# ScalarE issues the query/key weight loads and the gated stores, a SiLU moves behind the next copy, and one routing product is cut in two

## The chip, the cores and the metric

The kernel runs on one core of a Trainium2 chip. The metric is the device time of one execution in microseconds (us), lower is better. A profiled execution also gives a span, from the first to the last instruction that the profiler recorded; the time of that same execution is a little longer than its span.

## The reference, cut to what matters

All numbers are float32. The input `x` is 2 batches of 512 tokens with 512 features. A layer norm gives `xn`, and the output is

```
x + attention(xn) + mixture(xn)
attention: qkv  = silu(xn @ qkv_w.T)            # 32 heads, head size 128, q, k and v
           out  = a decayed linear attention: within a block  (q k^T * decay) v,
                  between blocks                              (q * q_decay) state,
                  state = state * block_decay + (k * k_decay)^T v
           gate = sigmoid(xn @ gate_w.T)
           y    = (gate * norm_w * out / rms(out)) @ out_w.T
mixture:   xn @ W_base.T + b_base, plus eight rank-16 experts, of which each token
           uses the two with the largest router value
```

## The kernel before, in words

**Stages.** A short setup normalises and transposes the tokens, computes the router and most of the base product, and prepares sums of input blocks. A long middle part, from about 26 us to about 940 us of the span, computes the four projections (v, gate, q, k) and, in its second half, the attention itself. The last part multiplies the gated attention with `out_w`.

**The projections are a two-level seven-product scheme.** A product of 2x2 blocks is made of 7 products of block sums instead of 8 products of blocks, and each of those 7 is again split into 7. One outer product is called a round, and it is one entry of the list `rounds`; one inner product is one slot, so that a round has seven slots. The list `SLOTS` says which inner product stands in which slot: `((0, 1), (0, 5), (1, 7), (0, 2), (0, 6), (0, 3), (1, 4))`. The first number tells whether it belongs to the current round or to the one before, the second is the number of the inner product. A slot costs TensorE about 0.86 us. Round kinds 0 and 1 compute v and gate; kind 2 computes queries and keys, for four heads in a set of weights. A set has seven rounds.

**What the other engines do for a round.** Inner product 1 is accumulated in the PSUM tile `pa` (a bank of the pair `fr`). Then ScalarE copies it to the tile `pb` (L558, `sd<-ps_fr` in the profile), because product 2 will be added on top of `pa` and product 6 on top of `pb`. Product 5 is made in `pc`, in the other bank of its pair. After product 6 ScalarE copies `pb` to `pd` (L569, `sd<-sd`), and VectorE takes `w` from `pb` (L552). Products 2, 3, 7 and 4 each end in an addition on VectorE (L537), whose result goes to an outer sum (`sum`) or, where the outer sum is complete, to the result itself. For queries and keys the result is the tile `qk`, and the function `result` then applies SiLU on ScalarE (L514), and calls `complete` when the item (one head of one batch) has all it needs.

**The attention of an item** is written as a generator, `attend`, and runs in pieces that the main loop starts in certain slots (`later`, `stage`): load v (L691), transpose keys by blocks on VectorE (L697, L698), store them to DRAM (L702, `k_kept`) and load them back in another layout by four loads (L707, `kt`), make the scores (L715, L720, L724), load the gate (L731), scale the keys on ScalarE (L736, `kd`), make the state (L739 to L746), make the output in PSUM and gate it (L756, `gT`), square it (L763, `sq`), and store it (L766, `g_kept`).

**The order is written by hand.** The middle part lies in a manual schedule: every engine executes its instructions in the order in which the Python code emits them, and each waits by semaphores for what it needs. SyncE (SP) has hardly any other work than to issue DMAs: each DMA is an instruction in its queue. Eight semaphores are shared by all DMAs, and each DMA waits for the earlier one on its own semaphore.

**Weight loads.** `load_block` fills a tile `raw` (five buffers) with two DMAs of 256 KB each, and the main loop takes one of them in every second slot of some rounds:

```
weights = load_blocks(n + 1, *{5: ((0, 0),), 7: ((1, 0), (1, 1)), 3: ((0, 1),)}.get(q, ()) ...)
if m % 2 == 0:
    next(weights, None)
```

The order within a slot is: weight load, delayed pieces (`later`), the piece of `stage`, the inner product of the slot, and then `after`, which emits the copies and additions that follow it.

Of the kernel before, what the change touches and what calls it, by code (L numbers as in the profile page):

```python
# [36 lines left out]
AF = mybir.ActivationFunctionType  # L37
# [5 lines left out]
P = 128  # L43
# [18 lines left out]
def attn_moe_kernel(ctx: ExitStack, tc: tile.TileContext, x, qk_w, v_w, gate_w, out_w, norm_w,  # L62
# [79 lines left out]
    def load_block(n, fo, ko):  # L142


        t = blocks[n, fo, ko] = aw.tile([P, 2, 2, 256], F32, tag="raw", name="raw", bufs=5)
        ks = slice(2 * ko, 2 * ko + 2)
        for i in range(2):
            if kind(n) == 0:
                nc.sync.dma_start(t[:, i], v_w[n - n % 2 + i][:, ks, fo * 256 : (fo + 1) * 256])
            elif kind(n) == 1:  # L150
                h = 4 * (n - n % 2) + 4 * i + 2 * fo
                nc.sync.dma_start(t[:, i], gate_w[h : h + 2, :, ks, :].rearrange("f p k d -> p f (k d)"))
            else:
                nc.sync.dma_start(t[:, :, i, :],
                                  qk_w[4 * (n - VG) + 2 * fo + i][:, :, ks, :].rearrange("p u k d -> p u (k d)"))
            yield

    def load_blocks(n, *of):
# [276 lines left out]
    def inner_product(o, r, i, first):  # L435
        n, q = rounds[r]
        a = operand[n, q][i]
        x_ = {1: xo[q][:, 0, :HB], 2: xo[q][:, 1, :HB], 3: xo[q][:, 1, HB:], 4: xt[q - 1][:, 3],
              5: xt[q - 1][:, 0], 6: xt[q - 1][:, 1], 7: xt[q - 1][:, 2]}[i]
        for u in range(2):  # L440
            if kind(n) == 0:

                mm(o.rearrange("p (g j d) -> p j g d", g=2, j=2)[:, u], x_[:, u * P : (u + 1) * P], a,
                   first and u == 0, True, turned=u, skip_group_check=True)
            else:
                mm(o[:, u * HB : (u + 1) * HB], a[:, u], x_, first and u == 0, True, skip_group_check=True)
# [59 lines left out]
    def result(n, fo, to, ij, v):  # L506

        fi, ti = divmod(ij, 2)
        if kind(n) < 2:
            g = pass_result(n, fo, to, ij, v)  # L510
            for slots in (3, 4):
                later[now[0] + slots].append(g)
            return
        nc.scalar.activation(v, v, AF.Silu)  # L514
        if ij in (1, 2):
            complete((4 * (n - VG) + 2 * fo + fi, to))

    def after(r, i):

# [66 lines left out]
    def route():  # L586

        f = work.tile([P, 4, NT, NE], F32, tag="squares", name="squares", bufs=2)
        g = work.tile([P, 8, NT], F32, tag="kd", name="kd", bufs=2)
        lg, prio, hit1, hit2 = (f[:, i] for i in range(4))  # L590
        c1, m1, m2, c2, w1, w2 = (g[:, i] for i in range(6))
        hl = moe["hl"] = ring("qk", [P, NT, NE, R])
        nc.sync.dma_start(lg, routed[:, :, :NE])
        nc.sync.dma_start(hl, routed[:, :, NE:].rearrange("p t (e r) -> p t e r", e=NE))
        yield

        for e in range(NE):
            nc.gpsimd.memset(prio[:, :, e : e + 1], float(NE - e))

        def wide(v):  # L600
            return v.unsqueeze(2).to_broadcast([P, NT, NE])

        def largest(m, c, hit):
            nc.vector.tensor_reduce(m, lg, AX.X, ALU.max)
            yield
            nc.vector.tensor_tensor(hit, lg, wide(m), ALU.is_equal)
            yield
            nc.vector.tensor_tensor(hit, hit, prio, ALU.mult)
            yield
            nc.vector.tensor_reduce(c, hit, AX.X, ALU.max)  # L610
            yield
            nc.vector.tensor_tensor(hit, hit, wide(c), ALU.is_equal)
            yield

        yield from largest(m1, c1, hit1)
        nc.vector.scalar_tensor_tensor(lg, hit1, LOWEST, lg, ALU.mult, ALU.add)
        yield
        yield from largest(m2, c2, hit2)

        nc.vector.tensor_tensor(w2, m1, m2, ALU.subtract)  # L620
        nc.scalar.activation(w2, w2, AF.Tanh, scale=0.5)
        for _ in range(4):
            yield
        nc.vector.tensor_scalar(w1, w2, SCALING / 2, SCALING / 2, ALU.mult, ALU.add)
        nc.vector.tensor_scalar(w2, w2, -SCALING / 2, SCALING / 2, ALU.mult, ALU.add)
        yield
        nc.vector.tensor_tensor(hit1, hit1, wide(w1), ALU.mult)
        yield
        nc.vector.tensor_tensor(hit2, hit2, wide(w2), ALU.mult)
        yield  # L630
        nc.vector.tensor_tensor(hit1, hit1, hit2, ALU.add)
        yield
        hl = hl.rearrange("p t e r -> p (t e) r")
        nc.vector.tensor_tensor(hl, hl, hit1.rearrange("p t e -> p (t e)").unsqueeze(2).to_broadcast([P, NT * NE, R]),
                                ALU.mult)

    def transpose_experts():

# [38 lines left out]
    def complete(item):  # L677

        items.append(item)
        g = running[len(items) - 1] = attend(*item)  # L680
        ready[len(items) - 1] = now[0] + 4
        for slots in (1, 2, 3, 6):
            later[now[0] + slots].append(g)

    def attend(head, b):
# [77 lines left out]
            nc.scalar.activation(sq, pa, AF.Square)  # L763
            nc.gpsimd.tensor_tensor(ssq[b], ssq[b], sq, ALU.add)  # L764
        yield
        nc.sync.dma_start(g_kept[head // 2][:, :, head % 2, b, :], gT.rearrange("p (f s) -> p f s", f=2))  # L766
        yield

    running = {}
# [124 lines left out]
    for k in range(7 * len(rounds) + 7):  # L894
        now[0] = k
        r0, m = divmod(k, 7)
        if m == 0:
            if r0 == 3:
                routing = route()
            if r0 == 15:  # L900
                for slots, g in zip((2, 5, 11, 18), 4 * [transpose_experts()]):
                    later[k + slots].append(g)
            if r0 == 50:
                zero_scores()
            if 20 <= r0 < 40:
                next(laying)
            if r0 in range(18, 18 + 3 * NT, 3):
                for slots, g in zip((0, 8, 11, 13), 4 * [experts((r0 - 18) // 3)]):
                    later[k + slots].append(g)
            if r0 + 2 < len(rounds):  # L910
                coming = encode(*rounds[r0 + 2])
            if r0 < len(rounds):
                n, q = rounds[r0]
                state_of[r0] = {}
                for _, to in ADDED[q]:
                    if to == "u3":
                        outer_sums[n, to] = outer_sums[n, "u2"]
                    elif isinstance(to, str):
                        if (n, q) == (1, 1):

                            t = [ring("qk", [P, 2, 512]) for _ in range(2)]
                            outer_sums[n, to] = [t[ij // 2][:, ij % 2] for ij in range(4)]
                        else:
                            t = aw2.tile([P, 4, 512], F32, tag="sum", name="sum", bufs=3)
                            outer_sums[n, to] = [t[:, ij] for ij in range(4)]
                weights = load_blocks(n + 1, *{5: ((0, 0),), 7: ((1, 0), (1, 1)), 3: ((0, 1),)}.get(q, ())
                                      if n + 1 < NSET else ())
        next(more_sums, None)

        if (r0, m) == (3, 0) or r0 in (5, 11, 12, 13):  # L930
            next(routing, None)
        if m % 2 == 0:
            next(weights, None)

        for g in later.pop(k, ()) if k != 7 * len(rounds) + 5 else ():
            next(g)
        begin_output(k - 7 * len(rounds))
        if r0 == len(rounds) and SLOTS[m][0] == 0:
            if m == 0:
                sums[0].update({1: bank("fr"), 6: bank("fr"), 5: seeded[0], 7: seeded[1]})  # L940
            early_product()
        begun = None
        if items:
            credit = min(credit + 24 / 49, 1.5)
            if credit >= 1:
                begun = next(stage)
        back, i = SLOTS[m]
        r = r0 - back
        if 0 <= r < len(rounds):
            st = state_of[r]  # L950
            if i in (1, 5):
                st["pa" if i == 1 else "pc"] = bank(
                    "at" if i == 5 and rounds[r] == (VG, 7) else "fr" if kind(rounds[r][0]) == 2 or i == 1 else "sc")
            inner_product(st[{1: "pa", 2: "pa", 5: "pc", 3: "pc", 6: "pb", 7: "pd", 4: "pd"}[i]], r, i, i in (1, 5))
            after(r, i)
        if r0 + 2 < len(rounds):
            next(coming, None)
        if begun is False:
            next(stage)
            credit -= 1  # L960
# [206 lines left out]
```

## Time and profile before

| | |
|---|---|
| three timed runs | 1118.1, 1119.52 and 1120.59 us, median 1119.52 us |
| profiled execution | 1121.18 us, its span 1119.4 us |
| mean granted TensorE clock | 0.998 |
| busy, share of the span | TensorE (PE) 1106.9 us, 99%; VectorE (DVE) 773.3 us, 69%; ScalarE (ACT) 444.9 us, 40%; GpSimd (POOL) 765.7 us, 68% |
| DMA issues by SP | 949, of which 64 are the query/key loads (L154) and 64 the `g_kept` stores (L766) |
| moved by DMA | 201.09 MB, mean 180 GB/s |

In the profile PE is TensorE's matrix multiply, PEld its weight load, DVE is VectorE, ACT is ScalarE, POOL is GpSimd and SP is SyncE; an engine's name with a q behind it is its instruction queue (its sequencer). L154 means line 154 of the kernel. Tile names stand without buffer numbers, `out<-in`. TensorE's busy time is modelled and matmuls overlap, so its waits are better read from the start times of successive products than from the busy share.

### The profile page before, as it was taken

How to read it: one execution, taken by the hardware profiler on the slowest of the kernel's cores; microseconds unless marked ns; L12 is line 12 of the kernel's file. 1: busy time of each engine (PE TensorE's matmuls, PEld its weight loads, DVE VectorE, ACT ScalarE, POOL GpSimd, SP SyncE). 2: the span in 40 equal slices, each digit the busy share in tenths (PEclk: the TensorE clock that was granted, in tenths of full speed). 3: DMA queues.
4: the chain of work that ended last, by engine and by line, in shares of the span. 5: the costliest groups of instructions: out<-in, count | busy, mean ns of one | idle time of the engine just before them, and what ended most of it. 6: DMA issues, size and time to landing. Idle time of an engine off the chain costs nothing.

```text
span 1119.4 us, 30341 instructions
## 1 busy us (share of the span) xinstructions
PE 1106.9 (99%) x11984; PEld 849.9 (76%) x11984; DVE 773.3 (69%) x1535; ACT 444.9 (40%) x842; POOL 765.7 (68%) x825
## 2 busy tenths in 40 slices
PE   8999999999999999999999899999999999999998
PEld 7666777777777777777777678777777877777776
DVE  8777776676766668787877777778777786535424
ACT  4344444434444444444444443535444443410000
POOL 3568778779768776677687676777777667545542
PEclk9999999999999999999999999999999999999999
DMA  5534576776743546665665666657666677944221
GB/s 178 156 114 159 163 241 202 220 229 209 239 143 132 177 146 197 182 199 154 199 187 160 191 183 186 189 164 211 181 197 177 211 234 233 350 132 127 86 90 57
DMA packets 190925, 201.09 MB, mean 180 GB/s; under 512 B 53696, under 2 KB 163008, under 8 KB 190656
## 3 DMA queue, kind: packets, MB, share of 16 engines
q1 hardware_dynamic: 190640, 199.03, 57.9%
q8 instruction: 95, 1.56, 0.6%
q14 instruction: 46, 0.38, 0.1%
q10 hardware_dynamic: 144, 0.13, 0.0%
HBM read 128.79 MB, written 75.55 MB: 183 GB/s over the span
## 4 chain that ended last, share of the span: by engine, by line
PE 79%; DVE 10%; DMA 4%; issue 3%; ACT 3%; SPq 1%; POOL 1%; DVEq 0%; ACTq 0%; POOLq 0%
PE sd L99 28%; PE ps_fr L99 24%; PE ps_sc L99 17%; PE ps_at L99 8%; PE ps_sc L715 2%; DVE qk L537 2%; DVE sum L537 2%; DMA raw<-in_qk_w 1%; ACT sd L569 1%; ACT qk L514 1%; DVE w L552 1%; DMA k_kept<-squares 1%; DMA v<-v_kept 1%; DVE gT L756 1%; DVE y L552 0%
## 5 line engine op out<-in xcount | busy, mean ns | idle before, releaser
L99 PE MATMUL sd<-xt,e 128*64 128x256 f32 x1344 | 175.8, 379 | 0.0
L764 POOL TENSOR_TENSOR ssq<-ssq,sq 128x512 f32<-128x512 f32 x62 | 79.2, 1277 | 138.0 <-ACT sq L763 131.0
L514 ACT ACTIVATE qk<-qk 128x512 f32<-128x512 f32 x128 | 80.3, 630 | 203.5 <-DVE qk L537 203.5
L99 PEld LDWEIGHTS sd<-xt,e 128*64 128x64 f32 x1344 | 102.6, 137 | 35.3 <-issue 2.6
L552 DVE TENSOR_TENSOR w<-sd,sum 128x512 f32<-128x512 f32 x110 | 74.5, 690 | 61.0 <-ACT sd L569 60.9
L569 ACT COPY sd<-sd 128x512 f32<-128x512 f32 x112 | 64.2, 573 | 130.1 <-PE sd L99 106.5
L558 ACT COPY sd<-ps_fr 128x512 f32<-128x512 f32 x112 | 64.2, 573 | 72.3 <-PE ps_fr L99 71.2
L99 PE MATMUL ps_at<-scores,v 128*64 128x128 f32 x1024 | 89.6, 273 | 0.0
L834 POOL TENSOR_TENSOR wsum<-wo 128x256 f32<-128x256 f32 x48 | 38.5, 821 | 68.7 <-PE sd L99 28.6
L833 DVE TENSOR_TENSOR gsum<-gated 128x256 f32<-128x256 f32 x54 | 27.3, 546 | 80.9 <-PE ps_sc L99 57.4
L172 POOL TENSOR_TENSOR s<-raw 128x1024 f32<-128x1024 f32 x32 | 75.7, 2367 | 6.8 <-DMA raw<-in_v_w 3.3
L99 PE MATMUL ps_at<-qd,state 128*64 128x128 f32 x768 | 75.2, 273 | 0.0
L99 PE MATMUL ps_fr<-xsum,s 128*64 128x256 f32 x576 | 75.1, 379 | 0.0
L99 PEld LDWEIGHTS ps_at<-scores,v 128*64 128x64 f32 x1024 | 65.9, 138 | 9.1 <-issue 0.4
L756 DVE SCALAR_TENSOR_TENSOR gT<-gate,ps_at 128x512 f32<-128x512 f32 x64 | 43.7, 682 | 36.1 <-PE ps_at L99 34.4
L727 POOL TENSOR_TENSOR qd<-qk,mask 128x384 f32<-128x384 f32 x64 | 64.7, 1010 | 0.9 <-PE ps_at L99 0.9
L191 POOL TENSOR_TENSOR e<-s 128x256 f32<-128x256 f32 x64 | 46.7, 730 | 23.7 <-PE sd L99 21.4
L715 PEld LDWEIGHTS ps_sc<-qk 128*64 128x64 f32 x1024 | 53.6, 137 | 8.7
L763 ACT ACTIVATE sq<-ps_at 128x512 f32<-128x512 f32 x62 | 37.0, 597 | 55.5 <-DVE gT L756 55.5
L99 PE MATMUL sd<-e,xt 128*64 128x256 f32 x448 | 59.0, 379 | 0.0
L99 PE MATMUL ps_fr<-xt,e 128*64 128x256 f32 x440 | 57.7, 382 | 0.2 <-DVE qk L537 0.2
L191 POOL TENSOR_TENSOR e<-raw 128x256 f32<-128x256 f32 x48 | 36.1, 753 | 30.7 <-PE sd L99 30.7
(349 smaller groups left out, 2959.6 us busy)
## 6 DMA issues: line engine op xcount, KB each, us to landing
raw<-in_qk_w SPq DMA_DIRECT2D x64, 256.0 KB
v<-v_kept SPq DMA_DIRECT2D x64, 256.0 KB
gate<-gate_kept SPq DMA_DIRECT2D x64, 256.0 KB
g_kept<-gT SPq DMA_DIRECT2D x64, 256.0 KB
gated<-g_kept SPq DMA_DIRECT2D x27, 512.0 KB
k_kept<-squares SPq DMA_DIRECT2D x64, 192.0 KB
kt<-k_kept SPq DMA_DIRECT2D x256, 48.0 KB
gate_kept<-v SPq DMA_DIRECT2D x47, 256.0 KB
```

The lines of the kernel that those rows point to most:

```text
L99: nc.tensor.matmul(o[h * HP : (h + 1) * HP], lhsT[:, of * HP : (of + 1) * HP], rhs, start=start, stop=stop, **more)
L172: nc.gpsimd.tensor_tensor(t, a, b, op)
L191: nc.gpsimd.tensor_tensor(e[:, 0], a21, a22, ALU.add)
L514: nc.scalar.activation(v, v, AF.Silu)
L537: engine.tensor_tensor(o, halves(v), halves(t), ALU.add)
L552: nc.vector.tensor_tensor(o, v, t, ALU.add)
L558: nc.scalar.copy(st["pb"], st["pa"])
L569: nc.scalar.copy(st["pd"], st["pb"])
L715: nc.tensor.matmul(pc[at * HP : (at + 1) * HP, asked], k[:, keys], q[:, asked], start=True, stop=True, skip_group_check=True)
L727: nc.gpsimd.tensor_tensor(qd, q[:, P:].rearrange("p (j n) -> p j n", j=TB - 1), mask[:, 3:5].rearrange("p h n -> p (h n)").unsqueeze(1).to ...
L756: nc.vector.scalar_tensor_tensor(gT, gate, 1.0, pa, ALU.add, ALU.mult)
L764: nc.gpsimd.tensor_tensor(ssq[b], ssq[b], sq, ALU.add)
```

## The change

Three things are changed, in four places of the code.

1. The DMAs of the query/key weights (L154) and the stores of the gated result (L766) are issued by ScalarE's queue instead of SP's. They stay where they were in the order of emission.
2. In `result`, the SiLU of quarter 2 of a result (which follows inner product 4, in the last slot of a round) is not emitted at once but put on a list `behind`. The main loop emits it in the next slot, after what `after` emits for inner product 1. `complete` is still called in the same slot.
3. In `route`, the product of the experts' hidden values with the routing weights, one VectorE instruction over 128x1024 elements (L634), becomes two over 128x512 with a slot between them.

```diff
@@ load_block
-                nc.sync.dma_start(t[:, :, i, :],
-                                  qk_w[4 * (n - VG) + 2 * fo + i][:, :, ks, :].rearrange("p u k d -> p u (k d)"))
+                nc.scalar.dma_start(t[:, :, i, :],
+                                    qk_w[4 * (n - VG) + 2 * fo + i][:, :, ks, :].rearrange("p u k d -> p u (k d)"))
@@ result
-        nc.scalar.activation(v, v, AF.Silu)
+        if ij == 2 and now[0] + 1 < 7 * len(rounds):
+            behind.append(v)
+        else:
+            nc.scalar.activation(v, v, AF.Silu)
         if ij in (1, 2):
             complete((4 * (n - VG) + 2 * fo + fi, to))
+
+    behind = []
@@ route
-        nc.vector.tensor_tensor(hl, hl, hit1.rearrange("p t e -> p (t e)").unsqueeze(2).to_broadcast([P, NT * NE, R]),
-                                ALU.mult)
+        for of in (slice(0, NT * NE // 2), slice(NT * NE // 2, NT * NE)):
+            nc.vector.tensor_tensor(hl[:, of], hl[:, of], hit1.rearrange("p t e -> p (t e)")[:, of].unsqueeze(2)
+                                    .to_broadcast([P, NT * NE // 2, R]), ALU.mult)
+            yield
@@ attend
-        nc.sync.dma_start(g_kept[head // 2][:, :, head % 2, b, :], gT.rearrange("p (f s) -> p f s", f=2))
+        nc.scalar.dma_start(g_kept[head // 2][:, :, head % 2, b, :], gT.rearrange("p (f s) -> p f s", f=2))
@@ main loop
             inner_product(st[{1: "pa", 2: "pa", 5: "pc", 3: "pc", 6: "pb", 7: "pd", 4: "pd"}[i]], r, i, i in (1, 5))
+            held_back = behind[:]
+            behind.clear()
             after(r, i)
+            for v in held_back:
+                nc.scalar.activation(v, v, AF.Silu)
```

## The prediction

> **What bounds the kernel now.** I read the engine table first, then TensorE's waits in the second half of the span, then the timelines around the changed places, and last what SP waits for.
>
> ```profile
> PE 1106.9 (99%) x11984; PEld 849.9 (76%) x11984; DVE 773.3 (69%) x1535; ACT 444.9 (40%) x842; POOL 765.7 (68%) x825
> ```
>
> ```profile
> PE ps_fr L99 <- ACT sd L558: 2.9, 8, 0.7
> PE ps_sc L99 <- ACT kd L736: 2.5, 1, 2.5
> ```
>
> TensorE never runs out of work for long. From 26 us on, the start times of successive products exceed their normal distance (0.86 us) by some 10 us in all. A change here can win only by closing those holes, and loses whatever new hole it opens. The waits name two kinds (us in total, times, longest): eight waits for the copy of `pa` (L558) and one for the scaled keys (`kd`). The timeline shows the first kind (start, duration, instruction, idle time before it):
>
> ```profile
> 764.50 0.63 ACT L514 ACTIVATE qk<-qk 128x512 f32<-128x512 f32 x1 [2.20 <-DVE qk L537]
> 765.70 0.63 ACT L514 ACTIVATE qk<-qk 128x512 f32<-128x512 f32 x1 [0.57 <-DVE qk L537]
> 766.24 0.58 ACT L558 COPY sd<-ps_fr 128x512 f32<-128x512 f32 x1
> 765.50 1.06 PE L99 MATMUL sd<-xt,e 128*64 128x256 f32 x8
> 766.87 1.08 PE L99 MATMUL ps_fr<-xnT,raw 128*64 128x256 f32 x8 [0.31 <-ACT sd L558]
> ```
>
> ScalarE waits for VectorE to end a round's last quarter, does its SiLU, and only then makes the copy. Product 2 starts 1.37 us after product 5, not 0.86: 0.51 us are lost. This recurs at 498.7, 564.6, 630.5, 700.9, 766.9, 832.8 and 898.7 us. The eighth wait, at 423.80 (0.91 us), stands behind a SiLU of quarter 1, which the change does not move.
>
> The second kind is in the chain of waits, at the last of the slow SP turns:
>
> ```profile
> 632.74 2.27 DMA kt<-k_kept
> 635.12 0.52 ACT kd L736
> 635.68 0.95 PE ps_sc L99 x12
> ```
>
> SP's own waits:
>
> ```profile
> SPq L707 <- DMA k_kept<-squares: 134.2, 54, 5.4
> ```
>
> SP's issues by source line (least, median and longest ns), and the table of windows around the hole (busy time of each engine, granted clock, DMA share, GB/s):
>
> ```profile
> L766 SPq DMA_DIRECT2D g_kept<-gT x64: 513/519/1236, 433.7 to 938.7; - x64
> L154 SPq DMA_DIRECT2D raw<-in_qk_w x64: 539/548/1441, 360.3 to 823.7; - x64
> ```
>
> ```profile
> 629.00:641.00 12.00, 9.19 (x94) 6.29 (x92) 5.77 (x15) 5.38 (x11) 9.73 (x9) 0.86 0.64 198
> ```
>
> SP runs late here: the stores of keys are issued at 602.6, 614.2 and 624.5 us, and each time SP waits for the landing (to 608.7, 618.8, 631.4) before it can issue the key loads; weight loads and `g_kept` stores stand in the same queue. TensorE loses 2.7 us, and in these 12 us its granted clock is 0.86 (1.00 in the 12 us before and after). Half a clock for some 3.4 us is 2.0 us more. The hole costs 4.7 us.
>
> **The change part by part.** The base is the profiled execution, 1121.18 us: 1.66 above the median of the runs, 1119.52. About 0.2% (2.2 us) is what a measurement of this kernel can tell from no change.
>
> *The SiLU of quarter 2.* It leaves the place ahead of L558, so the copy goes as soon as product 1 is done: 7 x 0.51 = -3.6 us. The SiLU itself now starts one copy (0.58 us) later or more; behind it stand VectorE's transposes of the same keys. VectorE is busy 77% of a set of weights, and the next use of those keys on TensorE lies over a slot away, so I cost this at nothing; without that cover it would be 0.6 us in each of the seven.
>
> *The routing product.* The hole at 125.27 us (0.5 us) comes from here: TensorE waits for a copy, that copy for a tanh, that for an addition at 123.31, and that for this instruction:
>
> ```profile
> 122.14 1.24 DVE L634 TENSOR_TENSOR qk<-qk,squares 128x1024 f32<-128x1024 f32 x1
> 125.27 1.08 PE L99 MATMUL ps_sc<-e,xnT 128*64 128x256 f32 x8 [0.31 <-ACT y L550]
> ```
>
> Halved, the second half goes behind the addition, which starts about 0.6 us earlier: -0.5 us.
>
> *What SP loses.* 128 issues of 0.52 to 0.55 us. An item takes 8.24 us, of which SP has about 4.9 us of issues and 2.5 to 5 us of waiting for `k_kept`. It gains 0.5 us an item everywhere, and 1.1 and more where weight loads stand too. From 602 to 635 us that is more than the 2.7 us of lateness: I take the hole to be gone, -4.7, and 0.2 off a smaller one at 916.5. At the other end of the bound the hole stays (0), since the store-to-load latency itself is unchanged.
>
> A rule speaks against this part. The Trainium skill, "DMA: Bandwidth & Descriptors", section "Issuing engines are not separate DMA queues", says that a second issuing engine saves only the sequencer's time to start a DMA, usually small beside the DMA itself. Here the row has that time at 0.52 us and SP's waits at 134.2 us, so by the rule alone the -4.7 would be near 0; the row decides only because lateness had added up over several items.
>
> *What ScalarE gains.* The same 128 issues. The only DMA that ScalarE issued before took 0.41 us, as SP's at the same moment did (0.40), so I use SP's 0.52 each. Can they pass while ScalarE waits? Of 215 semaphore rows of ScalarE that follow a compute instruction that had idled over 0.3 us, 214 start only after that instruction has started. So a DMA behind a waiting SiLU goes out from the SiLU's start: one hides under its 0.63 us, a second does not. The order of instructions after the change has SiLU, weight load, `g_kept` store, then the copy of `pb` (L569) at six places (483, 549, 615, 686, 751, 817 us). Before:
>
> ```profile
> 750.81 0.63 ACT L514 ACTIVATE qk<-qk 128x512 f32<-128x512 f32 x1 [1.05 <-DVE qk L537]
> 751.35 0.58 ACT L569 COPY sd<-sd 128x512 f32<-128x512 f32 x1
> 751.96 1.29 DVE L552 TENSOR_TENSOR w<-sd,sum 128x512 f32<-128x512 f32 x2 [1.18 <-ACT sd L569]
> 754.72 0.68 DVE L537 TENSOR_TENSOR qk<-ps_fr,w 128x512 f32<-128x512 f32 x1
> ```
>
> The copy would start at 750.81 + 2 x 0.54 + 0.04 = 751.93, 0.58 us later. VectorE waits for it (1.18 us idle) and then works back to back to the addition at 754.72, which frees the bank that TensorE fills at 755.54; all of it is late: 6 x 0.58 = +3.5 us. Before the copy L558 of the next slot stand two weight loads, with 0.75 us of room at six places (nothing) and none at 423.17: +0.6. Single stores ahead of L569 or L558 cost 0.04 to 0.1 us each: +0.5 for eight. Late stores (920 to 932 us), each waiting for the earlier DMA on its semaphore, stand ahead of squares and `kd`: 0 to 1.0, I take 0.4.
>
> The Trainium skill, "Perfetto Trace Analysis", part on the DVE and Act engine instruction, has a waiting instruction sit in a wait queue of its own while the sequencer goes on with the next; by that the DMAs would leave during the wait, and the sum would be 4 us lower. The 214 of 215 rows say otherwise for this engine.
>
> *Waits for a semaphore of a DMA.* Each DMA waits for the one eight or so earlier on its semaphore, and on ScalarE everything queued behind it waits too: SiLUs, the copies L558 and L569, the squares, `kd`, and so TensorE. By the landings of before (weight loads 4.7 to 5.3 us after issue, stores 3.6) most of these are over: at 549.2 the last landing is 548.96, at 751.4 it is 751.11. The trace does not show such a wait on ScalarE; bounds 0 and 1 us at each of seven tight places; I take +0.5 in all, near the landings shown.
>
> *Sum:* -3.6 - 0.5 - 4.7 - 0.2 + 3.5 + 0.6 + 0.5 + 0.4 + 0.5 = -3.5, so 1117.7 us against the profiled execution. Whether its 1.66 us over the median come back is open: the hole may have been smaller in the timed runs, or profiling adds time. Between 1117.7 and 1119.52 - 3.5 = 1116.0 I take 1117.0.
>
> **The rivals.**
>
> *The issues cost ScalarE nothing* (faster by more). For it: ScalarE is busy 40%, and where an instruction did not wait, 64 of 192 semaphore rows start ahead of its predecessor's start, so its queue can run ahead. Against it: the 214 rows above. Then +3.5, +0.6 and +0.5 fall away: -8.1 us, 1111.4 to 1113.1; if half is hidden, 1115.
>
> *ScalarE is blocked by its DMAs* (slower). The mechanism: a weight load at the head of ScalarE's queue waits for its semaphore, because the DMA eight earlier lands late, and the copy L569 or L558 behind it comes late. Place: the dense stretch of each set and the last item of it, 483 to 899 us. Price: with DMAs landing 1 us later than shown, or taking 1.2 to 1.4 us to issue as the longest rows do, 1 us more at each of the two tight slots of six sets, 12 us on top of the 1117, less what SiLU moves keep: 1122 to 1129. It decides from about 0.25 us a place on. For it: landings scatter (up to 6.5 us for weights), and 605 to 636 us would have waits of 0.8 to 3.9 us by before's landings. Against it: SP being less late, the earlier DMAs also leave sooner.
>
> *The hole returns elsewhere.* If the key latency and not SP's queue sets it, -4.7 is lost: 1122, no measurable change or slightly slower. *The SiLU move does nothing* if the copy then waits for VectorE through the order of banks; VectorE's bank waits (0.15 us at 764.6 and its like) are near: 1120.
>
> **How the numbers follow.** Forecast (with its neighbours, 1115.0 to 1119.4): 0.45, of which 0.24 faster, 0.19 same, 0.02 slower. Issue hidden: 0.25, all faster. ScalarE blocked, or the hole back: 0.30, of which 0.04 same and 0.26 slower. Faster 0.49, same 0.23, slower 0.28. Range: leaving out about one in ten on each side, 1111.8 to 1124.0.
>
> **What would show it.** Right: product 2 starts 0.86 us after product 5 at the seven places; no hole at 635 and no granted clock under 0.95 there; L569 some 0.6 us behind the SiLU's start plus its length at six places, with TensorE waiting there for a bank (DVE `qk` L537) by that much; the addition at 123 us is 0.6 us earlier. Wrong: L569 as early as before (issues hidden); rows of ScalarE's queue that wait for a DMA at L154 or L766; a wait for `kd` in the 600s or 900s; over 1 us of waits for L558 or L569 in each set.

## The result and the profile after

| | before | after |
|---|---|---|
| median of eight runs | 1118.01 us (1116.66 to 1120.59) | 1122.28 us (1118.82 to 1126.06) |
| ratio, 95% interval | | 1.0034 [1.0019, 1.0048] |
| profiled execution, span | 1121.18, 1119.4 us | 1121.97, 1120.2 us |
| delays of TensorE's products over 0.1 us, 400 to 940 us, summed | 11.5 us | 11.1 us |

The change makes the kernel 0.34% slower. (A delay is the distance between the starts of successive matmuls beyond the usual distance for their shape.) The two profiled executions differ by less than the medians: the one of before lies 3.2 us above its median and held a hole that the prediction put at 4.7 us; a second profile of that kernel, shown below, has no hole at that place, and 8.5 us in all by the count of the last row. Three parts of the prediction can be read at once in the waits of TensorE, 400 to 930 us (total, times, longest), after:

```profile
PE ps_fr L99 <- DVE qk L542: 4.0, 8, 0.6
PE ps_sc L99 <- ACT kd L743: 1.8, 1, 1.8
PE ps_fr L99 <- ACT sd L563: 1.5, 1, 1.5
```

(The lines of the kernel have shifted: the copy of `pa` is L563, of `pb` L574, `w` is L557, the addition of quarters L542, the SiLU L517 and, where it is held back, L966; `kd` is L743, `sq` L770, the gated store L773, the key load L714.) The eight waits for the copy of `pa` have become one, the one at 426 us that the SiLU move does not reach. In their stead TensorE waits for VectorE's addition, at six places of the same kind and two others. ScalarE, VectorE and TensorE at one of six such places show why:

```profile
749.10 0.63 ACT L517 ACTIVATE qk<-qk 128x512 f32<-128x512 f32 x1 [0.99 <-DVE qk L542]
749.11 0.57 ACTq L154 DMA_DIRECT2D raw<-in_qk_w  x1
749.72 0.63 ACTq L773 DMA_DIRECT2D g_kept<-gT  x1
750.45 0.57 ACT L574 COPY sd<-sd 128x512 f32<-128x512 f32 x1 [0.71 <-PE ps_fr L99]
```

```profile
751.05 1.29 DVE L557 TENSOR_TENSOR w<-sd,sum 128x512 f32<-128x512 f32 x2 [1.98 <-ACT sd L574]
753.81 0.68 DVE L542 TENSOR_TENSOR qk<-ps_fr,w 128x512 f32<-128x512 f32 x1
```

```profile
754.63 1.08 PE L99 MATMUL ps_fr<-xt,e 128*64 128x256 f32 x8 [0.59 <-DVE qk L542]
```

The first DMA goes out 0.01 us after the start of the SiLU that had been waiting, and hides under it; the second ends at 750.35, and only then comes the copy: 1.35 us after the SiLU's start, 0.54 before. The label on the copy's idle time (a product of TensorE) misleads: what it stood behind is the row above it. VectorE waits 1.98 us for the copy where it waited 1.18, its chain of additions follows without a gap, and TensorE's product is 0.76 to 0.80 us late at 489.9, 556.0, 622.4, 688.5, 754.6 and 821.1 us.

ScalarE's queue holds 19 such pairs of issues behind a waiting SiLU in this trace; besides these six, only the pair at 424 us costs TensorE anything, since at the other twelve the copy behind has room. The two other waits (0.35 us at 565 and 0.54 at 764 us) stand behind an addition of VectorE (`qk<-w,sum`) that took 1.48 and 1.68 us where it takes 1.29 before. It is drawn out (1.40 us and more) in six of the seven traces with the weight loads on ScalarE and in none of the six without; why is open.

The part that was meant to win is there too. At the place shown before, the copy now comes ahead of the held-back SiLU, and product 2 starts 0.87 us after product 5 (1.37 before):

```profile
764.56 0.58 ACT L563 COPY sd<-ps_fr 128x512 f32<-128x512 f32 x1
765.22 0.63 ACT L966 ACTIVATE qk<-qk 128x512 f32<-128x512 f32 x1
```

```profile
765.02 1.06 PE L99 MATMUL sd<-xt,e 128*64 128x256 f32 x8
765.89 1.06 PE L99 MATMUL ps_fr<-xnT,raw 128*64 128x256 f32 x8
```

The wait for `kd` is a hole of 2.05 us at 928 us:

```profile
924.80 0.60 ACT L770 ACTIVATE sq<-ps_at 128x512 f32<-128x512 f32 x1 [3.93 <-DVE gT L763]
926.95 0.52 ACTq L773 DMA_DIRECT2D g_kept<-gT  x1
927.65 0.80 ACT L743 ACTIVATE kd<-kt,mask 128x256 f32<-128x256 f32 x2 [2.25 <-DMA kt<-k_kept]
```

Between 924.80 and 926.95 ScalarE's queue stands at the store: it needs the semaphore of the store issued at 919.36, whose data landed only at 926.92. The key loads of this `kd` had left SP at 916.73 and had landed by 920.08; the release that the profile names is a later item's loads. SP's own queue, at last, waits no less (134.2 us in the first profile of before, 123.3 in the second):

```profile
SPq L714 <- DMA k_kept<-squares: 145.7, 54, 5.3
```

### The profile page after: what moved, and what is told of

Same layout as the page of the kernel before. It is cut to its first block, busy times and chain, and to the rows that moved or that the text cites. A ratio compares the mean times of both kernels' runs of the same rounds, so it can differ in the third digit from the quotient of the medians.

```text
span 1120.2 us, 30312 instructions
## 1 busy us (share of the span) xinstructions
PE 1106.3 (99%) x11984; PEld 842.7 (75%) x11984; DVE 771.6 (69%) x1536; ACT 444.1 (40%) x842; POOL 767.1 (68%) x825
## 4 chain that ended last, share of the span: by engine, by line
PE 89%; DVE 6%; ACT 1%; issue 1%; DMA 1%; ACTq 0%; POOL 0%; SPq 0%; DVEq 0%; POOLq 0%
PE sd L99 30%; PE ps_fr L99 28%; PE ps_sc L99 17%; PE ps_at L99 9%; PE ps_sc L722 3%; DVE qk L542 1%; DVE sum L542 1%; PE ps_sc L95 1%; DMA kt<-k_kept 1%; PE sd L95 1%; ACT sd L574 1%; ACT qk L517 1%; DVE w L557 0%; PE ps_fr L275 0%; DVE scores L731 0%
## 5 line engine op out<-in xcount | busy, mean ns | idle before, releaser
L517 ACT ACTIVATE qk<-qk 128x512 f32<-128x512 f32 x98 | 61.6, 630 | 157.7 <-DVE qk L542 152.9
L557 DVE TENSOR_TENSOR w<-sd,sum 128x512 f32<-128x512 f32 x110 | 74.5, 690 | 65.1 <-ACT sd L574 65.0
L574 ACT COPY sd<-sd 128x512 f32<-128x512 f32 x112 | 64.1, 573 | 130.1 <-PE sd L99 105.9
L563 ACT COPY sd<-ps_fr 128x512 f32<-128x512 f32 x112 | 64.1, 572 | 127.8 <-PE ps_fr L99 103.4
L99 PE MATMUL ps_at<-scores,v 128*64 128x128 f32 x1024 | 92.6, 273 | 0.0
L99 PE MATMUL ps_at<-qd,state 128*64 128x128 f32 x768 | 78.6, 273 | 0.0
L99 PEld LDWEIGHTS ps_at<-scores,v 128*64 128x64 f32 x1024 | 69.9, 137 | 6.7 <-ACT sq L770 0.2
L770 ACT ACTIVATE sq<-ps_at 128x512 f32<-128x512 f32 x62 | 37.1, 598 | 51.9 <-DVE gT L763 51.7
```

The source lines that it names most:

```text
L99: nc.tensor.matmul(o[h * HP : (h + 1) * HP], lhsT[:, of * HP : (of + 1) * HP], rhs, start=start, stop=stop, **more)
L557: nc.vector.tensor_tensor(o, v, t, ALU.add)
L563: nc.scalar.copy(st["pb"], st["pa"])
L574: nc.scalar.copy(st["pd"], st["pb"])
```

## The experiments

The first four take the parts one by one, against the kernel before; its median beside them is 1118.24 us.

**The SiLU move alone.** Edit: `result` and the main loop as in the change, nothing else.

```diff
+        if ij == 2 and now[0] + 1 < 7 * len(rounds):
+            behind.append(v)
```

> The kernel before with only the SiLU of quarter 2 moved behind the copy of pa. Theory A (ScalarE's DMA issues make the change slow, the SiLU move is a gain): the seven holes of 0.51 us close, about 3.6 us faster than before. Theory C (the moved SiLU delays VectorE's transposes and the keys, and pays back what it gains): within 1 us of before, with new waits for kd or for the addition behind the transposes.

Measured 1115.17 us, ratio 0.9971 [0.9958, 0.9984]: 3.1 us faster. The seven holes are closed. Holes for `kd` remain (0.89, 0.51, 1.42 and 0.88 us at 509, 706, 838 and 927 us); the kernel before has such holes too, of 4.7 us in one profile and 1.8 in another, so this run can't say whether the later SiLU adds to them. With 3.1 of 3.6 us gained, theory C falls. Of the eight waits for the copy of `pa` between 400 and 930 us one is left:

```profile
PE ps_fr L99 <- ACT sd L563: 0.6, 1, 0.6
```

**Both kinds of DMAs alone.** Edit:

```diff
-                nc.sync.dma_start(t[:, :, i, :],
+                nc.scalar.dma_start(t[:, :, i, :],
...
-        nc.sync.dma_start(g_kept[head // 2][:, :, head % 2, b, :], ...
+        nc.scalar.dma_start(g_kept[head // 2][:, :, head % 2, b, :], ...
```

> The kernel before with only the two kinds of DMAs on ScalarE's queue. Theory A: six places where TensorE waits 0.6 us more for VectorE, 0.75 us more at 424 us, up to 2 us for kd near 928 us, and the seven holes of 0.51 us are still there or larger, since two weight loads stand ahead of the copy too: 7 to 9 us slower than before (change 4.3 slower, plus the 3.6 that the SiLU move gave). Theory C: about as slow as the change, 4 us.

Measured 1126.16 us, 1.0065 [1.0045, 1.0085]: 7.9 us slower. The trace has six holes of 0.82 to 0.86 us, the seven of 0.52 us, 0.43 at 898 us, 1.72 at 425 us and 2.77 us at 932 us. With the move's 3.1 us and the routing product's 0.4 taken off, 4.4 us are left; the whole change measured 4.3.

**One kind of DMA each.** Edits: the first or the second half of that diff.

> The kernel before with only the query/key weight loads on ScalarE's queue. Theory A (one issue hides under the 0.63 us SiLU, two do not): the six late copies of pb before the 0.78 us waits come no more than 0.1 us late, and what is left is the pairs of weight loads ahead of the copy of pa, 0.5 us each at most: 0 to 4 us slower than before. Rival (any DMA behind a waiting SiLU delays the copy by its whole length): the six waits stay at 0.5 us or more.

> The kernel before with only the gated stores on ScalarE's queue. Theory A: a single store hides under the SiLU, so the six waits are absent; near 928 us the hole for kd (2.05 us in the change) appears if the stores or the freed SP queue cause it: 0 to 2 us slower than before. Theory B (the loss is one of transfers that now crowd, not of ScalarE's issue): the hole at 928 us is there, and the sum is as slow as the change, 4 us.

Weight loads alone: 1120.15 us, 1.0014 [1.0003, 1.0026], 1.9 us slower. Gated stores alone: 1121.86 us, 1.0027 [1.0016, 1.0039], 3.6 us slower. The six places have shrunk to 0.16 to 0.18 us in the one (but for one of 0.81) and to 0.15 to 0.19 in the other. ScalarE with the weight load alone, at one of them:

```profile
751.13 0.63 ACT L514 ACTIVATE qk<-qk 128x512 f32<-128x512 f32 x1 [1.05 <-DVE qk L537]
751.14 0.55 ACTq L154 DMA_DIRECT2D raw<-in_qk_w  x1
751.78 0.57 ACT L569 COPY sd<-sd 128x512 f32<-128x512 f32 x1
```

One issue is covered by the SiLU: the copy comes 0.65 us after the SiLU's start, 0.11 later than with none. The parts sum to 5.5 us, together they cost 7.9. The rest, 2.4 us, is no larger than the three intervals together leave open; in the traces the pairs account for more: six holes, each some 0.6 us larger than the two kinds apart make it, are 3.6 us. What the loads alone cost is in their trace at other places: 0.8 us more at 425 us, where a pair of loads stands, 0.62 us at 766 behind a drawn-out addition, and 1.74 us for `kd` at 580. The one hole of 0.81 us, at 555.9, is the wait for a DMA's semaphore that the prediction had listed as tight: there the load goes out 0.64 us after its SiLU's start, at 551.05, when the load issued at 544.72 has landed (551.02). The stores alone also bring a hole near 930 us (2.02, and 0.78 ahead of it). Some 0.8 us stands there too where SP issues the stores (0.82 in the second profile of before, 0.88 with the SiLU move alone), so about 2 us of it go with the stores.

The next four are variants, beside a median of 1118.21 us for the kernel before.

**The change without its DMA part.** Edit: both kinds of DMAs back to `nc.sync`.

> The change with both kinds of DMAs back on SP's queue: SiLU move and halved routing product alone. Theory A (ScalarE's issues are the whole loss): 3 to 4 us faster than before, as the SiLU move alone was (3.1), with 0.2 to 0.5 us more from the routing product. Rival (the halved product costs VectorE as much as it gives): not faster than the SiLU move alone.

Measured 1114.74 us, 0.9958 [0.994, 0.9976]: 3.5 us faster than before. The routing product's 0.4 us on top of the move is within the error of two medians; in the trace its hole goes from 0.51 to 0.29 us. The change with its DMA part is 7.5 us slower than this kernel. Of the scattered holes for `kd` three are here between 400 and 930 us:

```profile
PE ps_sc L99 <- ACT kd L743: 1.8, 3, 1.0
```

**Weight loads behind the slot's copies.** Edit:

```diff
-        if m % 2 == 0:
-            next(weights, None)
...
             for v in held_back:
                 nc.scalar.activation(v, v, AF.Silu)
+        if m % 2 == 0:
+            next(weights, None)
```

> The change with one edit: a slot's weight load is emitted behind the slot's copy instead of ahead of its product, so the copies of pa and pb no longer stand behind a weight load; the same DMAs, still on ScalarE. Theory A (place in the queue, not the number of issues, makes the loss): the six holes of 0.78 us fall to 0.2 us, the one at 426 us to about 0.9, the one at 928 us stays: 4 to 5 us faster than the change, about 1117.5 to 1118.5. Rival (ScalarE's time or the transfers themselves are what is lacking): within 1 us of the change, 1122.

Measured 1121.11 us: 1.2 us below the change, not 4 to 5, and within the change's own spread. Theory A as it was put here is wrong: not the place ahead of the copy counts. The old six places are clean, but six new holes of 0.81 to 1.6 us stand some 10 us behind them (497, 563, 630, 696, 763, 829 us). ScalarE's timeline has six new pairs 4 to 5 us ahead of these, here one of them: a load from the slot before meets a store of the next one, again behind a waiting SiLU.

```profile
757.83 0.63 ACT L517 ACTIVATE qk<-qk 128x512 f32<-128x512 f32 x1 [1.25 <-DVE qk L542]
757.84 0.55 ACTq L154 DMA_DIRECT2D raw<-in_qk_w  x1
758.42 0.63 ACTq L773 DMA_DIRECT2D g_kept<-gT  x1
759.10 0.63 ACT L517 ACTIVATE qk<-qk 128x512 f32<-128x512 f32 x1 [0.64 <-DVE qk L542]
```

**The late stores back on SP.** Edit:

```diff
-        nc.scalar.dma_start(g_kept[...
+        (nc.scalar if now[0] < 7 * len(rounds) else nc.sync).dma_start(g_kept[...
```

> The change with the gated stores behind the last round (from about 912 us) issued by SP, all earlier ones by ScalarE. Theory A (the hole of 2.05 us at 928 us is the scaling of keys behind a store that waits for the semaphore of the store before it): the hole at 928 us is gone, the others stay: about 2 us faster than the change, 1120. Rival (the keys land late because transfers crowd there, whoever issues them): the hole stays at 1 us or more, and the time within 0.5 us of the change.

Seven of the 64 stores go back. Measured 1119.12 us, 3.2 us below the change and no different from before (0.9999 [0.9987, 1.0011]). The hole of 2.05 us is gone; one of 0.87 has come, for a later item's keys. The traces show 1.2 us of the 3.2 there; the rest is within the spread of the change's runs. In ScalarE's timeline the scaling now follows the squares at once, where 2.85 us lay between the two starts:

```profile
923.35 0.60 ACT L770 ACTIVATE sq<-ps_at 128x512 f32<-128x512 f32 x1 [4.16 <-DVE gT L763]
923.84 0.79 ACT L743 ACTIVATE kd<-kt,mask 128x256 f32<-128x256 f32 x2
```

**A best version.** SiLU move, halved product, weight loads on SP, and the stores as in the last diff.

> SiLU move and halved routing product, gated stores on ScalarE up to the last round and on SP behind it, weight loads on SP. If the holes for kd that come and go with SP's lateness (0.5 to 4.7 us in the traces that have both kinds of DMAs on SP) cost 1 to 2 us in the median run, and single stores 0.1 us each: 1 us faster than the SiLU move with the routing product, about 1114. If those holes are an accident of the profiled runs: no gain, or 0.5 us slower than that.

Measured 1113.2 us, 0.9952 [0.9936, 0.9967]: the fastest kernel here, 9.1 us below the change and 5.0 below before. TensorE's waits from 400 to 930 us have no `kd` any more:

```profile
PE ps_fr L99 <- ACT sd L563: 0.6, 1, 0.6
PE ps_fr L99 <- DVE qk L542: 0.2, 1, 0.2
```

SP's wait for `k_kept` falls to 98.3 us. The median is 1.5 us lower with 57 issues fewer on SP (1114.74 to 1113.20), where none is paired on ScalarE. With 8 and 6 runs whose ranges overlap (1112.09 to 1116.16, 1112.6 to 1114.98), that is not clear of noise; in the two traces the holes for `kd` over 0.3 us, 2.4 us in all, are gone.

The last three ask what was still open: whether the pair is the cause, whether the costs add up, and whether the hole at 635 us belongs to the kernel before. The median of before is 1118.01 us here.

**The pair taken apart.** One number of the change is edited; all 128 DMAs stay on ScalarE:

```diff
-        if m % 2 == 0:
+        if m in (0, 2, 5, 6):
             next(weights, None)
```

> The change with one number edited: a round's third weight load is taken in slot 5 instead of slot 4, so that it no longer stands with a gated store ahead of the copy of pb; all DMAs stay on ScalarE, none is left out. Theory A (only two issues behind one waiting SiLU delay the copy): the six holes of 0.78 us fall to 0.15 us, those at 426 us (1.66) and 928 us (2.05) stay: 3.5 to 4 us faster than the change, about 1118.5. Rival 1 (the loads make a new pair elsewhere, as when they were put behind the copies): six holes of 0.8 us at another place, 1121 to 1122. Rival 2 (ScalarE has no time for 128 issues, wherever they stand): within 1 us of the change.

Measured 1117.05 us: 5.2 us below the change, 0.9991 [0.9979, 1.0002] of before. The six holes are gone; 1.55 us at 425, 0.61 at 564 (behind a drawn-out addition again) and 1.47 at 923 us stay. Both rivals fall: no new pair costs anything, and the number of issues is not the cause. The waits for VectorE's addition (4.0 us, eight times, in the change), and ScalarE's timeline, one issue under the SiLU, the other under the copy:

```profile
PE ps_fr L99 <- DVE qk L542: 0.6, 2, 0.4
```

```profile
746.24 0.63 ACT L517 ACTIVATE qk<-qk 128x512 f32<-128x512 f32 x1 [0.98 <-DVE qk L542]
746.25 0.59 ACTq L773 DMA_DIRECT2D g_kept<-gT  x1
746.93 0.57 ACT L574 COPY sd<-sd 128x512 f32<-128x512 f32 x1
746.95 0.59 ACTq L154 DMA_DIRECT2D raw<-in_qk_w  x1
```

**Both edits.** The slots of the last version, the late stores on SP.

> The change with both edits: the third weight load in slot 5, and the gated stores behind the last round issued by SP. If the two costs are separate, the gains add up: 3.5 to 4 us below the 1119.1 of the version with the late stores on SP, about 1115.3, with 1.66 us left at 426 us. If one edit only moves the loss to the other's place: 1117 to 1119.

Measured 1115.74 us, 0.9976 [0.9966, 0.9985], 3.4 us below the version with the late stores alone on SP, as was expected of separate costs. The sum is not exact: apart the two edits gained 5.2 and 3.2 us, together 6.5. The gap of 1.9 us is of the size of the uncertainty of the change's median (its interval is 1.6 us to each side).

**Before, profiled again.** No edit.

> The kernel before, unchanged, profiled once more. If the hole of 4.7 us at 635 us is an accident of the first profile (SP's lateness by landings that scatter), it is absent or at another place and of another size here, and the time is 1116.5 to 1118.5. If it belongs to the program: at 635 us again, 2 us or more, and 1121.

Measured 1120.94 us in this one execution. There is no hole at 635 us; there are 0.97 us at 842 and 0.82 us at 931 us, in the waits as

```profile
PE ps_sc L99 <- ACT kd L736: 0.7, 1, 0.7
```

So the hole at 635 us is an accident of the first profile; the traces of the SiLU move alone and of the change without its DMA part don't have it either. The time, expected at 1116.5 to 1118.5, is no smaller for another reason, a setup that took 2.3 us longer: the first of the seven holes, at 498.7 us in the first profile, is at 501.0 here.

## Why the prediction was wrong

The forecast was 1117.0 us and faster; it is 1122.28 and slower. The range held the time, the sign was wrong. The two parts that were meant to win did (3.5 us together, 4.1 forecast). The step that failed is the balance of moving the DMAs: +0.6 us in the sum (-4.9 for SP, +5.5 for ScalarE), +7.5 measured (1122.28 against 1114.74 without them). Its two main errors are a credit to SP that was not there, some 3.4 us, and ScalarE's costs, of which the late stores were 1.65 us too small and the pairs 0.8. By the steps of the sum:

- **The SiLU move** was right: 7 x 0.51 = 3.6 us forecast, 3.1 measured alone. VectorE does wait for the held-back SiLUs now (21.1 us, 22 times, before its transposes), and no hole of TensorE is put down to that wait; whether it feeds the scattered holes for `kd` was not separated.
- **The routing product**: 0.5 forecast, 0.22 us in the trace. The hole at 125 us (0.51) is gone, but the product after next now starts 0.29 us late, at 127.25 us. The prediction had not looked past the first hole.
- **What SP loses** is the step that failed most. The prediction took 4.7 us for a hole of one execution and made it a property of the kernel. In the second profile the holes for `kd` are 1.8 us, and freeing SP of 57 stores went with 1.5 us in the median, not clear of noise. The mechanism has something to it: the stores' place on SP decides whether such holes appear (last section). The profiled execution's excess over the median was a warning that the prediction saw and split the difference on. Its base was high besides: the median of eight runs is 1118.01, of the first three 1119.52. (The hole itself was nearer 4.5 us: the clock row has half a clock for 3.4 us, which is 1.7 and not 2.0 us, and from 630.55 to 700.95 us the set takes 70.40 us, its neighbours 65.92.) The Trainium skill, "DMA: Bandwidth & Descriptors", section "Issuing engines are not separate DMA queues", says that a second issuing engine saves only the usually small time of starting a DMA. The runs side with it more than the prediction did: 57 issues of 0.52 us are some 30 us of SP's time, against the 1.5 us in the median. SP's wait for `k_kept` tells little here: it is 145.7 us with 128 issues fewer, 146.6 with the SiLU move and no issue moved, and 98.3 with the 57 stores moved.
- **What ScalarE gains**: the mechanism was right to the place, one issue hidden and the second not. Its size was 0.58 us a place; measured were 0.78, or 0.71 more than the 0.07 that was there, because the two issues took 0.57 and 0.63 us where the working had 2 x 0.54, and 0.1 us passed before the copy: +4.3 for +3.5. At 426 us it was +0.75 for +0.6. Some 0.6 us more came from the drawn-out additions at 565 and 764 us, for which the sum had no term.
- **Late stores**: 0 to 1.0 us allowed, 0.4 taken, 2.05 in the trace; the run that took them off ScalarE was 3.2 us faster, 1.3 where the pairs had been taken apart first. The store's semaphore was that of a store 7.6 us earlier; the prediction had used before's landings, in which that wait was SP's and hurt nobody.
- **Waits for a DMA's semaphore in the tight places**: +0.5 taken. In the change there is none of weight: of 49 DMAs that directly follow, in the order of emission, a ScalarE instruction that had idled over 0.3 us, 48 start within 0.1 us of that instruction's start; the 49th is the store at 926.95. Before 900 us only the weight loads alone showed such a place with a price, the 0.81 us at 555.9.

The rival nearest to the result, "ScalarE is blocked by its DMAs", was put at 1122 to 1129 us, with a chance of 0.30 for it or the returning hole. Its cause was only half right: the issue time of the pairs made more of the loss than waits for semaphores, which did harm at one place, the end. The rival "the hole returns elsewhere" named 1122 us, by luck close: its -4.7 was indeed lost, but no hole for `kd` came back between 430 and 900 us, and other terms made up the time. The rival "the issues cost ScalarE nothing" fell: of those 49 DMAs none starts ahead of the waiting instruction. It holds where the instruction ahead had not idled (last section). The Trainium skill, "Perfetto Trace Analysis", part on the DVE and Act engine instruction, lets the sequencer go on while an instruction waits in the wait queue; at 749.10 and 749.11 us the row shows a DMA leaving only with the start of the SiLU ahead of it.

The prediction's signs of being right were all seen: 0.87 us from product 5 to product 2, no hole at 635 us and a clock of 1.00 there, the late copy at the six places, the earlier addition in the routing. Of its signs of being wrong it saw one, the wait for `kd` in the 900s. They tested the places one by one; none tested whether the credit of 4.7 us was there in the usual run.

## What to carry to other kernels

Before a DMA is moved to the queue of a computing engine, list what stands behind each issue there. In these traces one issue (0.52 to 0.6 us) behind a SiLU (0.63 us) that waits hides under it; two in a row delay what stands behind by the second's whole length, which costs only where that has no room (7 of 19 pairs). An issue that waits for an earlier DMA holds up everything behind it (2.15 us at 924.80), so stores that nobody needs soon do not belong ahead of work that TensorE waits for. And a hole that one profile shows is worth its price only if a second profile, or the spread of the timed runs, shows it too.

## What the runs showed that was not expected

An issue on ScalarE's queue is covered by the instruction ahead of it, a SiLU or a copy alike (749.11 under 749.10; 746.95 under 746.93), so the same 128 issues cost 7.5 us or 2.3 us (1122.28 and 1117.05 against 1114.74 without them), by one slot's shift of a round's third weight load.

The queue also runs ahead, in this trace only past instructions that had not idled: of 54 DMAs in the change that directly follow, in the order of emission, an instruction that had not idled over 0.3 us, 47 start ahead of it, by up to 1.57 us. Here the store stands behind the scaling of keys in the order of emission, and starts 1.16 us before it:

```profile
707.13 0.52 ACTq L773 DMA_DIRECT2D g_kept<-gT  x1
708.29 0.80 ACT L743 ACTIVATE kd<-kt,mask 128x256 f32<-128x256 f32 x2
```

The hole for `kd` is not fixed to a place: at 635 us in the first profile of before, at 842 and 931 in the second, at 509, 706, 838 and 927 us with the SiLU move alone; each of the five traces with the stores on SP has one, whoever issues the weight loads. With the stores of the middle part on ScalarE it was gone from 430 to 900 us in seven of eight traces (the eighth has 0.38 us).
